# Layer 1 of a four-layer image network: norm sums on 32-column tiles of ones, variances through DRAM, and a new order of work

## The chip, the cores and the metric

The kernel runs on one core of one Trainium2 chip. The metric is the device time of one execution in microseconds (us): the median of several runs, each timed as a whole. A core has five engines with a queue of instructions each: TensorE (PE, with the weight loads, PEld, shown apart), VectorE (DVE), ScalarE (ACT), GpSimd (POOL) and SyncE (SP). SP issues the transfers (DMAs) between DRAM and the on-chip memory. Matmuls write to the accumulation memory, PSUM; the other operands lie in SBUF, both with 128 partitions. An engine works through its queue in order, so an instruction that waits holds up everything queued behind it.

## The reference

Sixteen images of 96 channels and 56 x 56 = 3136 positions pass through four layers. Only the second of them, called layer 1, is touched. It normalises each position over its channels, projects to 192 channels, convolves, runs a selective scan in four directions, normalises again, projects back, and ends with a normalised two-layer perceptron:

```python
def _ln(x, g, b, eps=1e-05):
    m = x.mean(-1, keepdims=True)
    v = ((x - m) ** 2).mean(-1, keepdims=True)
    return (x - m) * jax.lax.rsqrt(v + eps) * g + b
...
z = jnp.transpose(x, (0, 2, 3, 1))
u = _ln(z, norm1_g, norm1_b)
u = u @ in_proj_w.T
...
dt = jax.nn.softplus(jnp.einsum('bkrl,kdr->bkdl', dts, dt_projs_w) + dt_projs_b[None, :, :, None])
a = jnp.exp(dt[:, :, :, None, :] * A[None, :, :, :, None])
bb = dt[:, :, :, None, :] * Bs[:, :, None, :, :] * xs[:, :, :, None, :]
...
_, h = jax.lax.associative_scan(comb, (a, bb), axis=-1)
...
ym = _ln(ym, out_norm_g, out_norm_b)
z = z + ym @ out_proj_w.T
m = _ln(z, norm2_g, norm2_b)
m = jax.nn.gelu(m @ fc1_w.T + fc1_b, approximate=False) @ fc2_w.T + fc2_b
z = z + m
return x + jnp.transpose(z, (0, 3, 1, 2))
```

There are thus three norms per image: the first over 96 input channels, the second over the 192 channels that come out of the scan, the third over 96.

## The kernel before

Layer 0, layer 1 and layers 2 and 3 run one after the other, with their images in DRAM in between. Layer 1 keeps channels in partitions for most of its work and treats one image after another, with neighbouring images overlapping. An image goes through these tasks:

- `front` loads the image in chunks of 896 columns (`loaded`, L1004). Its inner task `sums` squares each piece of 448 columns on ACT (L1029). It then takes 112 columns at a time as weights, with a block of 96 columns of ones/96 as the moving operand: `p_s` (L1035, L1036) holds the mean and the mean square of 112 positions, one position per partition, repeated 96 times. DVE copies out one column of each (L1038), two small operations make the variance (L1044, L1045) and POOL raises it to the power -1/2 (L1047). `projected` loads the chunk again. It spreads the roots over 96 partitions by 28 transposes of a broadcast column (`p_r`, L1057), multiplies (L1062), and projects (L1067). The convolution (L1107) and a silu (L1130) follow. Last, a small projection on four 32-column tiles (L1144, one of its three operands read with a step of 56 elements) is copied to `proj` (L1146), and its rows B and C go to DRAM (`bc`, L1150).
- `made_of` makes the step sizes and decays on PE (L1174) and ACT (L1181, L1183, L1190), and loads the rows of B and C from DRAM, broadcast to 128 partitions (L1203, three buffers `bc`).
- `scanned` is DVE's work: products (L1262, L1265), the scan itself (L1271, L1273) and the product with C (L1226, L1229), in 24 pieces of 784 columns per image. POOL adds directions together (L1295), and at the end DVE folds two halves (L1300). The results are two tiles of an image's size, `y0` (128 channels) and `ym` (64 channels).
- `back` works in seven groups of 448 positions, as three chains. A group squares y on ACT (L1317, L1319). With 112 columns of y as weights it computes the output projection plus one column of means (L1324, L1325), and with 112 columns of squares as weights against ones, the mean squares (L1327). ACT copies the projection out (L1332), DVE makes the variance (L1340, L1341), POOL the power (L1343), DVE scales (L1350) and adds the input image that PE has transposed (`p_y`, L1347, L1352). Then come the third norm (L1357 to L1368), a transpose (L1372), the perceptron (L1382, L1384, L1392, L1393), the last addition (L1395) and the store (L1397).

The order of all this is made by hand while the program is built. Each task is a generator that yields `Op`s: an engine, a guessed cost, a lag until the result can be used, and the buffers that it takes and gives back. `in_order` simulates the engines with these guesses and picks, again and again, the operation with the earliest possible start. Ties go first to an operation that frees PSUM, then to the lower rank. The ranks are `3 * b + -9` for fronts, -100 for `made_of`, 99 for the scan, -1 for the additions and `3 * b` for backs. The instructions are issued in the order of these picks, and on the chip each engine keeps to it. A scanning image and its neighbours share seven image-sized buffers (`big`), three PSUM buffers (`ps`) and single or double buffers of everything else.

```python
            if best is None or (start, rank) < best[:2]:
                best = (start, rank, i)
```

ACT holds one table of functions at a time. The tasks need those of exp (also ln), gelu and silu, and a change costs a table load.

Of the kernel before, what the change touches and what calls it, by code (L numbers as in the profile page):

```python
# [8 lines left out]
F32 = mybir.dt.float32  # L9
# [3 lines left out]
AF = mybir.ActivationFunctionType  # L13
# [150 lines left out]

class Phase:
# [60 lines left out]
def in_order(buffers, tasks, load=None):  # L226
# [8 lines left out]
    def advance(ready, task, parent, root):  # L235
        nonlocal count
        while True:
# [14 lines left out]
            elif isinstance(got, int):  # L252
                ranks[root] = got
            else:
                waiting.append((ready, ("ps" not in got.give, ranks[root], count), task, parent, got, root))
                count += 1
                return
# [3 lines left out]
    while waiting:  # L261
        best = None
        for i, (ready, rank, _, _, op, _) in enumerate(waiting):
            start = max(ready, engines.get(op.engine, 0.0))
            if op.engine == "ACT" and op.table and op.table != tables.get("ACT"):
                start = max(ready, engines.get("ACT", 0.0) + change["ACT"])
# [5 lines left out]
            if best is None or (start, rank) < best[:2]:  # L272
                best = (start, rank, i)
        start, _, i = best
        assert start < np.inf, "the tasks hold all buffers"
        _, _, task, parent, op, root = waiting.pop(i)
# [560 lines left out]
def layer1(ctx, tc, src, given, dst, flags=None, soft=False):  # L837
# [6 lines left out]
    buffers = {  # L844
        "ps": 3, "x": 1, "half": 1, "xc": 2, "big": 7, "proj": 2, "dt": 3, "a": 2, "bc": 3, "hc": 1, "xn": 1,
        "ysq": 1, "o": 2, "z": 2, "zn": 2, "zt": 1, "hid": 1, "xr": 3,
    }
# [28 lines left out]
    ones = ph.c([P, 3, C], "ones")  # L876
# [57 lines left out]
    for i in range(2):  # L934
# [11 lines left out]
        rows.append(ph.c([C1, C], f"rows{i}"))  # L946
        nc.vector.tensor_copy(rows[i], p[:C1, 0, :C])
# [4 lines left out]
    nc.vector.memset(w_out[:, 0, C:], 1.0 / DIN)  # L952
    nc.vector.memset(w_out[:64, 1, C:], 1.0 / DIN)
    for j, n in enumerate((P, 64)):
# [5 lines left out]
        nc.vector.tensor_copy(w_out[:n, j, :C], p[:n, 0, :C])  # L960
    b_fc1 = ph.c([P, 3], "b_fc1")
# [28 lines left out]
    def pe(n, each, take=("ps",), give=(), **k):  # L990
        return Op("PE", n * each, 0.25, take, give, **k)

    def dve(n, each=1.04e-3, over=0.15, **k):
        return Op("DVE", over + n * each, **{"lag": 0.06, **k})

    def act(n, each=0.83e-3, over=0.22, **k):
        return Op("ACT", over + n * each, **k)

    def front(b, it):

        def loaded(g):
            n = min(896, L - 896 * g)
            x = buf([C, 896], "xc")[:, :n]
            nc.sync.dma_start(x, given[b][:, 896 * g : 896 * g + n])  # L1004
            return x
# [15 lines left out]
        me = work.tile([Q, 8, NT], F32, tag="me", name="me")  # L1021

        def sums(g):
            yield Op("SP", 0.3, 4.0, take=("xc",))
            x = loaded(g)
            for i in range(x.shape[1] // T):
                yield act(T, take=("xn",))
                sq = buf([C, 2, T], "xn")[:, 0]
                nc.scalar.activation(sq, x[:, T * i : T * i + T], AF.Square)  # L1029
                last = i == x.shape[1] // T - 1  # L1030
                yield pe(8, 0.2, give=("xn", "xc") if last else ("xn",))
                p = pair("p_s", P)
                for q in range(4):
                    at = T * i + Q * q
                    nc.tensor.matmul(p[:Q, q, :C], x[:, at : at + Q], ones[:C, 0], start=True, stop=True)  # L1035
                    nc.tensor.matmul(p[:Q, 4 + q, :C], sq[:, Q * q : Q * q + Q], ones[:C, 0], start=True, stop=True)  # L1036
                yield dve(8, give=("ps",))
                nc.vector.tensor_copy(me[:, :, 2 * g + i : 2 * g + i + 1], p[:Q, :, 0:1])  # L1038

        yield [sums(g) for g in range(4)]  # L1040
# [837 lines left out]
```

## Time and profile before

| what | value |
|---|---|
| median of 3 runs | 7140.69 us |
| the 3 runs | 7134.35 to 7140.94 us |
| the profiled execution | 7114.45 us |
| its span, first to last instruction | 7112.6 us |
| PE busy | 6280.9 us (88%) |
| DVE busy | 5446.3 us (77%) |
| ACT busy | 4546.6 us (64%) |
| POOL busy | 1446.6 us (20%) |
| mean granted PE clock | 0.92 |
| DMA | 743.56 MB, mean 105 GB/s |

The durations in the prediction come from the one profiled execution. Busy time of an engine is the time in which at least one of its instructions runs. Matmuls overlap one another, so the mean duration of a matmul is longer than its share of PE's time; the distance from one start to the next is the better measure. A line such as `2217.64 0.36 PE L1035 ... x2` in the timeline gives the start, the length, and how many instructions were merged. A line of waits gives who waited for whom, the total in us, the number of times and the longest. In a line of stages, the busy us of each engine are followed by the number of its instructions, the granted PE clock, DMA's mean share and its GB/s.

### The profile page before, as it was taken

What the parts mean: (1) busy time and instruction counts of PE and PEld (TensorE: products, weight loads), DVE (VectorE), ACT (ScalarE), POOL (GpSimd) and SP (SyncE); (2) the same over time, 40 slices, a digit from 0 to 9 for tenths busy, and PEclk for the clock granted to TensorE, in tenths of its full rate; (3) what the DMA queues carried; (4) which work ended last, traced back from release to release, by engine and by line L of the source; (5) the groups of instructions that cost most, each with busy time, mean ns of one, the idle gap of its engine ahead of it and who ended that gap; (6) DMA issues with size and microseconds to landing.
All of it is one profiled execution on the core that took longest, in us unless ns stands there. A gap on an engine that the chain in (4) does not pass through costs nothing. (4 is left out here: it accounts for less than half of the span.)

```text
span 7112.6 us, 114994 instructions
## 1 busy us (share of the span) xinstructions
PE 6280.9 (88%) x46587; PEld 4500.6 (63%) x46587; DVE 5446.3 (77%) x7392; ACT 4546.6 (64%) x6035; POOL 1446.6 (20%) x994
## 2 busy tenths in 40 slices
PE   7999998888889999999999987788999999999986
PEld 3444444445655655556555555687888888888875
DVE  6786884677888888888888885667777777777775
ACT  4454542676777777777777763455666666666664
POOL 0000000132323333333333332111111111111110
PEclk9999998788899999999999988899999999999997
DMA  1111111343444444444444442445555455555542
GB/s 38 31 38 32 40 33 38 110 123 117 124 127 124 127 127 130 127 137 127 128 131 130 126 122 76 96 107 125 130 115 126 112 128 118 121 135 118 119 105 61
DMA packets 495422, 743.56 MB, mean 105 GB/s; under 512 B 199969, under 2 KB 330785, under 8 KB 491570
## 3 DMA queue, kind: packets, MB, share of 16 engines
q1 hardware_dynamic: 493858, 733.25, 39.9%
q8 instruction: 370, 6.06, 0.4%
q0 software_dynamic: 1024, 2.85, 0.1%
q14 instruction: 170, 1.39, 0.1%
HBM read 543.98 MB, written 191.99 MB: 103 GB/s over the span
## 5 line engine op out<-in xcount | busy, mean ns | idle before, releaser
L1578 POOL TENSOR_TENSOR r<-v,nhalf 112x16 f32<-112x16 f32 (+1 forms) x128 | 397.0, 3108 | 2241.5 <-DVE v L1576 1680.7
L1295 POOL TENSOR_TENSOR big<-big,hc 128x784 f32<-128x784 f32 x256 | 537.2, 2099 | 901.9 <-DVE hc L1226 815.2
L1262 DVE TENSOR_TENSOR dt<-dt,big 128x784 f32<-128x784 f32 x384 | 505.5, 1317 | 176.9 <-ACT a L1190 176.7
L777 DVE SCALAR_TENSOR_TENSOR h<-pad,rows,h 128x1568 f32<-128x1568 f32 x288 | 525.9, 1844 | 3.9
L1174 PE MATMUL p_d<-proj,l_dt 32*128 32x392 f32 x1536 | 388.3, 590 | 96.6 <-ACT hid L1384 69.1
L1181 ACT ACTIVATE dt<-p_d,l_dtb 128x784 f32<-128x784 f32 x384 | 350.0, 912 | 128.2 <-PE p_d L1174 110.6
L1636 PE MATMUL p<-k_f,z 112*128 112x112 f32 x3072 | 373.9, 282 | 63.9 <-DMA z<-d 57.5
L1636 PEld LDWEIGHTS p<-k_f,z 112*128 112x128 f32 x3072 | 369.2, 198 | 72.4 <-issue 59.1
L1684 PE MATMUL p_v<-w,gg 128*112 128x97 f32 x2048 | 377.3, 267 | 38.3 <-DVE gg L1670 12.3
L1107 PE MATMUL p_c<-x,taps 64*64 64x392 f32 x4608 | 400.7, 498 | 3.7 <-ACT big L1128 2.7
L1265 DVE TENSOR_TENSOR drive<-dt,bc 128x784 f32<-128x784 f32 x384 | 395.0, 1029 | 11.1 <-DMA bc<-bc 1.0
L1392 PE MATMUL p_g<-l_fc,hid 128*112 128x96 f32 x2688 | 386.1, 285 | 11.8 <-ACT hid L1384 9.4
L1128 ACT COPY big<-p_c 64x392 f32<-64x392 f32 (+1 forms) x448 | 267.3, 599 | 189.7 <-PE p_c L1107 184.1
L1392 PEld LDWEIGHTS p_g<-l_fc,hid 128*112 128x112 f32 x2688 | 347.2, 200 | 51.0 <-ACT hid L1384 24.6
L1685 PE MATMUL p_v<-w2both,gg 128*112 128x97 f32 x2048 | 375.5, 266 | 0.0
L1226 DVE TENSOR_TENSOR hc<-a,bc 128x784 f32<-128x784 f32 x384 | 371.3, 967 | 0.3 <-POOL big L1295 0.2
L1183 ACT ACTIVATE dt<-dt,one 128x784 f32<-128x784 f32 x384 | 363.6, 947 | 7.2
L1382 PE MATMUL p_f<-zt,w_fc 96*128 96x448 f32 x672 | 320.1, 594 | 47.6 <-ACT dt L1181 18.8
L1190 ACT ACTIVATE a<-dt,aneg 128x784 f32<-128x784 f32 x384 | 352.1, 939 | 4.5 <-DVE a L1273 3.1
L750 PE MATMUL p_c<-pad,taps 64*64 64x392 f32 x4032 | 348.8, 495 | 1.8 <-DVE y L816 1.4
L1273 DVE TENSOR_TENSOR_SCAN a<-a,drive 128x784 f32<-128x784 f32 x192 | 350.3, 1824 | 0.1
L1271 DVE TENSOR_TENSOR_SCAN a<-a,drive 128x784 f32<-128x784 f32 x192 | 350.0, 1823 | 0.0
(339 smaller groups left out, 16005.2 us busy)
## 6 DMA issues: line engine op xcount, KB each, us to landing
bc<-bc SPq DMA_DIRECT2D x256, 784.0 KB
bc<-bc SPq DMA_DIRECT2D x256, 392.0 KB
d<-y SPq DMA_DIRECT2D x448, 192.0 KB
z<-d SPq DMA_DIRECT2D x128, 672.0 KB
d<-uu SPq DMA_DIRECT2D x256, 169.8 KB
z<-d SPq DMA_DIRECT2D x192, 194.0 KB
xc<-x SPq DMA_DIRECT2D x96, 336.0 KB
x<-in_x SPq DMA_DIRECT2D x16, 1176.0 KB
```

Source lines behind the costliest of these rows:

```text
L777: nc.vector.scalar_tensor_tensor(out, view, taps9[:, i : i + 1], out, ALU.mult, ALU.add)
L1107: nc.tensor.matmul(p[to : to + 64, b, :TC], taps[64 * s : 64 * s + 64, j, k], pad[64 * s : 64 * s + 64, r0 : r0 + 7, k % 3 : k % 3 + S], s ...
L1174: nc.tensor.matmul(p[:, b, :TC], wdt[on, i], proj[on, h], start=True, stop=True)
L1226: nc.vector.tensor_tensor(hc, a, t[:, 1], ALU.mult)
L1262: nc.vector.tensor_tensor(as_own(dt), as_own(dt), own(u), ALU.mult)
L1265: nc.vector.tensor_tensor(b, dt, t[:, 0], ALU.mult)
L1295: nc.gpsimd.tensor_tensor(out, out, hc, ALU.add)
L1392: nc.tensor.matmul(p[:Q, q, :C], hid[:, j, own], fc2[:, j], start=j == 0, stop=False)
L1578: nc.gpsimd.tensor_tensor(r, v, nhalf[:, :n], ALU.pow)
L1636: nc.tensor.matmul(p[:, q, :Q], flat[:, P * (3 * q + k) : P * (3 * q + k) + P], f2, start=True, stop=True)
L1684: nc.tensor.matmul(out, gs[2 * h][:, at + k], w["w2"][:, 2 * h], start=True, stop=False)
L1685: nc.tensor.matmul(out, gs[1][:, at + k], w["w2both"][:, h], start=False, stop=True)
```

## The change

The first norm becomes a task of its own, `norms`, which writes the roots of an image to a row in DRAM, `root`; `fronts` waits for it. In both the first and the second norm, the block of ones becomes the weight: 32 columns of ones/n on one of four 32-column tiles of PE, with a quarter of the chunk (224, 112 or 196 columns) streaming through each. The sums then lie along the free dimension, the same value in 32 partitions. A new helper, `spread`, squares the means on ACT, makes the variance on DVE and writes one partition of each tile to a DRAM row. Once the row is complete it is loaded again with 28 values in each of 112 partitions, EPS is added and POOL makes all 3136 roots at once. The first norm's roots go back to DRAM and are loaded broadcast over 96 partitions (buffer `xr1`), so that the 28 transposes fall away. The second norm's stay in `r2`, where partition p holds the roots of positions 4p to 4p+3 of each group.

The groups of `back` follow that layout: `each` takes every fourth column of y0, ym and x as weights, so that one partition holds four neighbouring positions. The store then writes them as one piece (`"(p q) c -> p q c"`, before `"(q p) c -> p q c"`). The squares, the ones matmuls, the copy of the projection and the small variance operations leave the group, since the scaling by `r2` reads PSUM directly. `p_y` shares a PSUM tile with `p_o`. The 97th column of `w_out` and `rows` now holds row sums, so that the sum over channels of z comes out of the projection and the reduction L1359 falls away.

A table, TUNED, holds the counts of buffers, the ranks (fronts `3 * b - 6`, the new norms `3 * b - 6`, the scan -50), a handicap for an operation that would change ACT's table (`hold`, 0.7) and a bias in us for some pairs of engine and task (`leads`). `in_order` adds bias and handicap to the start when it picks, not to the simulated time. Some guessed costs change too.

```diff
+            'leads': {('PE', 'spreads'): -2.4,
+                      ('PE', 'steps'): -3.4,
+                      ('SP', 'sums'): -1.2,
+                      ('ACT', 'spreads'): -0.3,
+                      ('DVE', 'additions'): -0.2,
+                      ('ACT', 'hidden'): -0.7,
+                      ('SP', 'norms'): 1.6,
+                      ('POOL', 'fronts'): -0.9,
+                      ('DVE', 'some'): -0.3,
+                      ('POOL', 'norms'): 0.4,
+                      ('PE', 'some'): -0.6,
+                      ('ACT', 'sums'): 0.5,
+                      ('SP', 'projected'): -2.9,
+                      ('DVE', 'norms'): 0.1,
+                      ('POOL', 'backs'): -0.6},
+            'hold': 0.7, 'norm': -6, 'front': -6, 'back': 0, 'make': -100, 'scan': -50, 'chains': 3}}
...
-            start = max(ready, engines.get(op.engine, 0.0))
+            start, key = max(ready, engines.get(op.engine, 0.0)), leads.get((op.engine, name), 0.0)
             if op.engine == "ACT" and op.table and op.table != tables.get("ACT"):
-                start = max(ready, engines.get("ACT", 0.0) + change["ACT"])
+                start, key = max(ready, engines.get("ACT", 0.0) + change["ACT"]), key + hold
...
-            if best is None or (start, rank) < best[:2]:
-                best = (start, rank, i)
+            if best is None or (start + key, rank) < best[:2]:
+                best = (start + key, rank, i, start)
...
-        "ysq": 1, "o": 2, "z": 2, "zn": 2, "zt": 1, "hid": 1, "xr": 3,
+            'ysq': 1, 'vr': 2, 'xr1': 1, 'z': 2, 'zn': 1, 'zt': 1, 'hid': 1, 'xr': 2},
...
+    def spread(mean, square, out, n):
+        yield act(n, take=("vr",))
+        t = buf([P, 224], "vr")[:, :n]
+        nc.scalar.activation(t, mean, AF.Square)
+        yield dve(n, give=("ps",))
+        nc.vector.scalar_tensor_tensor(t, t, -1.0, square, ALU.mult, ALU.add)
+        yield Op("SP", 0.3, 3.0)
+        nc.sync.dma_start(out.rearrange("o (q n) -> (o q) n", q=4), t[::32])
+        yield Op("none", 0.0, 0.0, give=("vr",))
...
+    def normed(b, it):
+        var, it["root"] = (dram.tile([1, L], F32, tag=n, name=n) for n in ("var", "root"))
+        def sums(g):
+            yield Op("SP", 0.3, 4.0, take=("xc",))
+            x = loaded(b, g)
+            n = x.shape[1] // 4
+            yield act(4 * n, take=("xn",))
+            sq = buf([C, 896], "xn")[:, : 4 * n]
+            nc.scalar.activation(sq, x, AF.Square)
+            yield pe(2, n * 1.7e-3, give=("xn", "xc"))
+            p = pair("p_s")
+            for k, a in enumerate((x, sq)):
+                for q in range(4):
+                    nc.tensor.matmul(
+                        p[32 * q : 32 * q + 32, k, :n], ones[:C, 0], a[:, n * q : n * q + n], start=True, stop=True
+                    )
+            yield from spread(p[:, 0, :n], p[:, 1, :n], var[:, 896 * g : 896 * g + 4 * n], n)
...
         def projected(g):
...
-                nc.tensor.transpose(
-                    p[:C, q // 4, Q * (q % 4) : Q * (q % 4) + Q], r[:, at : at + 1].to_broadcast([Q, C]), ident[:Q, :Q]
-                )
-            yield dve(448 * banks, give=("ps", "xc"))
-            nc.vector.tensor_tensor(xn, x.rearrange("c (b n) -> c b n", n=T), p[:C, :banks, :T], ALU.mult)
+            nc.sync.dma_start(rb, it["root"][:, 896 * g : 896 * g + n].to_broadcast([C, n]))
+            yield dve(448 * banks, take=("xn",), give=("xr1", "xc"))
+            nc.vector.tensor_tensor(xn.rearrange("c b n -> c (b n)"), x, rb, ALU.mult)
...
+        def spreads(g):
+            cols = slice(SUB * g, SUB * g + SUB)
+            yield act(SUB, take=("ysq",))
+            sq = buf([P, SUB], "ysq")
+            nc.scalar.activation(sq, y0[:, cols], AF.Square)
+            yield act(SUB)
+            nc.scalar.activation(ym[64:, cols], ym[:64, cols], AF.Square)
+            yield pe(4, n * 1.7e-3, give=("ysq",))
...
+            yield from spread(p[:, 0, :n], p[:, 1, :n], var[:, cols], n)
...
+        each = lambda t, q: t.rearrange("c (p q) -> c q p", q=4)[:, q]
...
-            yield pe(16, 0.2, ("ps", "o"), ("ysq",))
+            yield pe(8, 0.2, ("ps",))
             p = pair("p_o", P)
             for q in range(4):
-                nc.tensor.matmul(p[:Q, q, :C1], y0[:, own], w_out[:, 0], start=True, stop=False)
-                nc.tensor.matmul(p[:Q, q, :C1], ym[:, own], w_out[:, 1], start=False, stop=True)
...
+                nc.tensor.matmul(p[:Q, q, :C1], each(y0[:, cols], q), w_out[:, 0], start=True, stop=False)
+                nc.tensor.matmul(p[:Q, q, :C1], each(ym[:64, cols], q), w_out[:64, 1], start=False, stop=True)
...
+                nc.tensor.matmul(p[:Q, 4 + q, :C1], each(x, q), rows[0], start=True, stop=True)
...
+                z, p[:Q, :4, :C1], r2[:, 4 * g : 4 * g + 4].unsqueeze(2).to_broadcast([Q, 4, C1]), ALU.mult
...
-        in_order(buffers, [fronts(), makes(), scans(), additions(), backs()], None if soft else one_set)
+        in_order(buffers, [norms(), fronts(), makes(), scans(), additions(), backs()], None if soft else one_set, tuned["hold"], tuned["leads"])
```

## The prediction

> **What bounds the kernel now.** I first cut the span into stages. Layer 1 runs from 1152 us, where layer 0 ends, to 4417 us. The busy time by stage shows its head (first image only), its steady part and its tail:
>
> ```profile
> core 0: us, PE busy (x) PEld busy (x) DVE busy (x) ACT busy (x) POOL busy (x), PEclk, DMA share, GB/s
> 1152.00:1282.00 130.00, 96.43 (x704) 59.60 (x704) 14.80 (x61) 37.39 (x51) 12.60 (x29) 0.71 0.11 31
> 1282.00:4085.00 2803.00, 2518.66 (x18722) 1602.23 (x18722) 2365.01 (x2807) 2117.83 (x2752) 902.67 (x644) 0.90 0.44 128
> 4085.00:4417.00 332.00, 272.14 (x1722) 208.97 (x1718) 244.24 (x349) 190.26 (x267) 99.99 (x76) 0.86 0.32 89
> ```
>
> The copy of `proj` (L1146) ends each image's front: its first start is 1281.6 us, its sixteenth 4085.3, so one image takes 2803.7/15 = 186.9 us. The stretch 2007 to 4077 us has PE busy 1899.7, DVE 1791.6 and ACT 1602.0 of 2070 us. That is 171.5, 161.8 and 144.6 us per image, or 92%, 87% and 77% of the period. PE is nearest to full, and DVE is close behind.
>
> Next, what DVE waits for in that stretch, since the scan runs there:
>
> ```profile
> DVE z L1395 <- PE p_g L1393: 115.8, 65, 12.5
> DVE dt L1262 <- ACT a L1190: 79.2, 35, 4.6
> ```
>
> These are 195 of 278 us of DVE's idle time. The first is a wait on PE. The second is a wait on ACT, which itself waits most for PE (p_c 118.1, p_o 103.6, p_d 58.3 us). So PE's load and the hand-made order of the three engines set the period together.
>
> Last, PE's pace. The groups overstate short matmuls, which overlap, so I read starts in the timeline:
>
> ```profile
> 2217.64 0.36 PE L1035 MATMUL p_s<-ones,xc 96*112 96x96 f32 x2
> 2217.83 0.36 PE L1036 MATMUL p_s<-ones,xn 96*112 96x96 f32 x2
> 2218.03 0.36 PE L1324 MATMUL p_o<-w_out,big 128*112 128x97 f32 x2
> 2218.23 0.36 PE L1325 MATMUL p_o<-w_out,big 128*112 128x97 f32 x2
> ```
>
> Each fp32 matmul is two instructions, and the next one starts 0.195 us later: 0.098 us per instruction with its own load of 112 weight columns. After a PE gap the same pair takes 0.37 us (2254.50 to 2254.87) at clock 0.50.
>
> The third reading is what a strided operand costs PE. L1144 runs four 32-column tiles side by side, contiguous ones and ones that read with a step of 224 bytes:
>
> ```profile
> 1278.91 0.12 PEld L1144 LDWEIGHTS p_x<-big,l_xw 128*32 128x32 f32 x4 [0.37 <-issue]
> 1279.24 0.12 PEld L1144 LDWEIGHTS p_x<-big,l_xw 128*32 128x32 f32 x4 [0.21 <-issue]
> 1279.94 0.14 PEld L1144 LDWEIGHTS p_x<-big,l_xw 128*32 128x32 f32 x4 [0.58 <-issue]
> 1280.66 0.14 PEld L1144 LDWEIGHTS p_x<-big,l_xw 128*32 128x32 f32 x4 [0.58 <-issue]
> ```
>
> A new row marks the start of a pass of 392 columns. The contiguous pass took 0.33 us (0.84 ns per column, for four tiles at once), the two strided ones 0.70 and 0.72 us (1.8 ns).
>
> [...] No strided weight load is in this trace. [...] Here the first `bc` rows went to DRAM from 1282.4 and were in use at 1290.3 us, so a write and a read together took at most 7.9 us.
>
> **The change, part by part** (per image, at full clock).
>
> PE, removed: 56 sums matmuls (L1035, L1036) x 0.195 = 10.9 us; 28 transposes of r (L1057, eight instructions in 0.8 us) = 5.6; 56 ones matmuls in the back (L1327) x 0.195 = 10.9. Together 27.4 us.
> PE, added: 32-column tiles in sets of four. The first norm streams 784 columns per tile for x and again for its square; the second 784 for each of two halves of y and their squares. (2+4) x 784 x 2 passes x 0.84 ns = 7.9 us. If the weight loads don't hide, perhaps 12.
> PE, slowed: `each` takes every fourth column, so y0, ym and x are now weights with a step of 16 bytes. Per group that is 8 (p_o) + 4 (p_y) + 4 (L1393) = 16 matmuls, so 32 instructions, and 224 per image. [...]
> Net for PE: -27.4 + 7.9 + 20 = about 0 (bounds -20 and +10).
>
> DVE, removed: seven copies (L1038) 1.15, L1044 and L1045 0.4, L1340 and L1341 (22.2 + 17.7)/16 = 2.5, the reduction L1359 60.8/16 = 3.8. Added: eight `spread` operations on 224 or 196 columns, by the 384-column row of 0.55 us about 0.35 each = 2.8, and two of 28 elements, 0.4. The other two passes over z grow by one column in 97. Net -4.6 us.
>
> ACT, removed: L1332 53.1/16 = 3.3, squares (64.0 + 63.9 + 63.6)/16 = 12.0. Added: four squares of 896 (3.6), eight of 784 (7.4), eight of the means (0.35 each, 2.8). Net -1.5. There are 124 + 111 + 16 = 251 table loads of 1.283 us, 20 us per image. `hold` and `leads` weigh when they come. I take a gain of 1 us of period from order and tables together; bounds -5 to +5, because the trace can't show an order that doesn't exist yet.
>
> POOL: seven powers of 1.39 become one, taken like L1047's 5.1: -4.7, and POOL is 33% busy. The row sums at setup are a few instructions, nothing.
>
> SP and DMA: 15 more DMAs per image (8 row writes, two reads of variances, one write and four broadcast reads of roots), at about 0.4 us of issue = 6 us. SP's existing waits come to about 160 us per image, nearly all for a buffer to come free. Data: 1.2 MB more of broadcasts on DMA engines at 45%. [...] Costed at nothing: three `bc` buffers lie ahead of DVE, which waited 1.0 us for them in all of layer 1. The added waits sit in SP's queue, though: a read of `var` or `root` waits until the write has landed, and the next `bc` rows queue behind it, and L1265 on DVE behind those.
>
> Head: about 33 us from the first p_s (1180) to the first xn (1213) at low clock. Afterwards four loads, three DRAM trips and the power, about 28: -5. Tail: the spreads and the trip come before the last image's first group, about +25 after 4325; each group then loses two squares, a copy, two small operations and a power, some 6 us in 2.3 rounds, and p_o waits less: -20. Together 0.
>
> **Sum.** DVE's 4.6 us less, at its 87% share, shortens the period by 5.3; with 1 for order about 6 us. 15 x 6 = 90. The profiled execution took 7114.45 us (span 7112.6): 7024. The runs' median lies 26 us above it, so 7050.
>
> **Rivals.**
> A, strided weights load at full pace. [...] PE falls to 171.5 - 27.4 + 7.9 = 152 us, DVE at 157.2 becomes the bound; its best long windows show 91.5%, so 172 us: -15 x 15 = -225, 6915.
> B, the slower one: strided loads cost more than L1144's pace. At 0.25 us a load PE gains 30 instead of 20, so +10, 181.5 us. At today's 92% the period is 197: +10 x 15 = +150, 7290. It decides from a load of about 0.23 us on: the forecast's period of 180.9 already has PE at 95%, and at 0.23 (25 gained, 177) PE needs the old period at that share. Against it: the measured strided pace gives 0.20.
> C, SP blocked by the DRAM trips: three per image, 3 us of DVE wait each beyond the cover gives +9 - 6 = +3, +45: 7185. Against it: 1.0 us of wait today.
> D, what goes comes back as other waits: 7140.
>
> **Chances.** Forecast 0.40 (own range 6970 to 7150, 0.05 of it slower), A 0.27, B 0.16, C 0.10, D 0.07. A measurement can tell about 0.2%, 14 us. Faster 0.35 + 0.27 = 0.62, same 0.07, slower 0.05 + 0.16 + 0.10 = 0.31. Range 6850 (A with DVE at 95%) to 7250.
>
> **What would show it.** The distance between weight loads of p_o: 0.1 us gives A, 0.2 the forecast, over 0.23 B. A pass of the new p_s near 0.19 us for 224 columns. DVE near 157 us per image. Waits of L1265 on DMA over 100 us would give C. The forecast falls if the period in the steady part is below 176 or above 187.

## The result, and the profile after

The changed kernel takes 7614.95 us (median of 4 runs, 7610.44 to 7622.51). The kernel before, run beside it, takes 7138.89. The ratio is 1.067, with an interval of 1.065 to 1.0687: 476 us slower, far outside the forecast's range.

The stages of layer 1 in the kernel after (head left out; then steady part, tail, and a stretch inside the steady part):

```profile
core 0: us, PE busy (x) PEld busy (x) DVE busy (x) ACT busy (x) POOL busy (x), PEclk, DMA share, GB/s
1275.00:4452.00 3177.00, 2930.81 (x17758) 1700.63 (x17750) 2274.84 (x2491) 2008.73 (x2557) 803.56 (x553) 0.78 0.40 116
4452.00:4927.00 475.00, 396.72 (x1736) 279.93 (x1734) 285.73 (x349) 206.43 (x264) 110.43 (x77) 0.67 0.28 80
1990.00:4109.00 2119.00, 1981.37 (x11684) 1186.76 (x11681) 1518.46 (x1697) 1326.10 (x1693) 549.23 (x378) 0.79 0.40 115
```

The copies of `proj` (now L1201) start at 1275.0 us for the first image and at 4451.7 for the sixteenth, so the period is 211.8 us instead of 186.9. That makes 15 x 24.9 = 373 us. From the sixteenth copy to the last addition (L1465, at 4921.2) it is 469.5 us instead of 331.3, another 138. The first copy starts 7 us earlier. Together 505 us, of which the span shows 497; the rest is in the other layers.

PE is busy 93.5% of the third stretch. DVE's 1518.46 of 2119 us at this period are 151.8 us per image, fewer than the 161.8 of before: DVE has less to do and waits for PE. The granted clock fell from 0.90 to 0.78. The waits of DVE and ACT between 2000 and 4000 us confirm who is late (total in us, times, longest):

```profile
ACT dt L1236 <- PE p_d L1229: 229.0, 83, 9.7
DVE z L1465 <- PE p_g L1463: 178.8, 59, 6.1
DVE z L1419 <- PE p_o L1416: 150.8, 63, 6.8
DVE dt L1317 <- ACT a L1245: 101.4, 45, 6.0
```

The first was 58.3 us before and is now the longest wait of either engine: the step sizes, on which the scan depends, wait behind PE's other work. The third belongs to an addition that waits for the slowed matmuls themselves.

The pace of these matmuls in the timeline, at full clock until 2018.4 us:

```profile
2010.95 1.70 PE L1122 MATMUL p_in<-xn,w_in 96*128 96x448 f32 x4
2012.48 0.45 PE L1408 MATMUL p_o<-w_out,big 128*112 128x97 f32 x2
2012.86 0.65 PE L1409 MATMUL p_o<-w_out,big 64*112 64x97 f32 x2
2013.44 0.65 PE L1408 MATMUL p_o<-w_out,big 128*112 128x97 f32 x2
2014.02 0.65 PE L1409 MATMUL p_o<-w_out,big 64*112 64x97 f32 x2
...
2016.90 1.97 PE L1416 MATMUL p_o<-rows,xr 97*112 97x97 f32 x8
2018.80 1.68 PE L1229 MATMUL p_d<-proj,l_dt 32*128 32x392 f32 x4
2020.40 3.36 PE L1122 MATMUL p_in<-xn,w_in 96*128 96x448 f32 x4
```

From one start of p_o to the next it is 0.58 us for two instructions, so 0.29 us for each; before it was 0.098. The eight loads of x in L1416 take 1.9 us here and 1.65 us at 2057.69, 0.21 to 0.24 us each. Then something shows that the forecast had no term for: the same four instructions of p_in that took 1.70 us at 2010.95 take 3.36 us at 2020.40. The clock dropped to 0.5 while PE had not been idle for a moment:

```profile
2011.00:2018.30 7.30, 7.30 (x28) 5.88 (x27) 3.74 (x5) 3.34 (x5) 6.18 (x2) 1.00 0.47 146
2018.40:2032.00 13.60, 13.16 (x26) 5.60 (x27) 10.28 (x13) 7.53 (x9) 5.14 (x4) 0.50 0.34 110
```

### The profile page after: what moved, and what is told of

Same layout as the page of the kernel before. It is cut to its first block, busy times and chain, and to the rows that moved or that the text cites. A ratio compares the mean times of both kernels' runs of the same rounds, so it can differ in the third digit from the quotient of the medians.

```text
span 7609.6 us, 112950 instructions
## 1 busy us (share of the span) xinstructions
PE 6789.7 (89%) x45627; PEld 4641.1 (61%) x45627; DVE 5398.6 (71%) x7074; ACT 4458.3 (59%) x5845; POOL 1358.0 (18%) x898
## 5 line engine op out<-in xcount | busy, mean ns | idle before, releaser
L1317 DVE TENSOR_TENSOR dt<-dt,big 128x784 f32<-128x784 f32 x384 | 481.1, 1253 | 186.5 <-ACT a L1245 185.0
L1229 PE MATMUL p_d<-proj,l_dt 32*128 32x392 f32 x1536 | 453.9, 685 | 83.4 <-ACT hid L1454 43.2
L1462 PE MATMUL p_g<-l_fc,hid 128*112 128x96 f32 x2688 | 485.6, 336 | 8.8 <-ACT hid L1454 6.8
L1462 PEld LDWEIGHTS p_g<-l_fc,hid 128*112 128x112 f32 x2688 | 439.0, 247 | 52.5 <-ACT hid L1454 34.5
L1452 PE MATMUL p_f<-zt,w_fc 96*128 96x448 f32 x672 | 373.7, 681 | 34.8 <-ACT zt L1445 14.2
L1320 DVE TENSOR_TENSOR drive<-dt,bc 128x784 f32<-128x784 f32 x384 | 380.0, 989 | 10.3
L1682 PE MATMUL p_a<-first,xt 97*112 97x192 f32 x1792 | 334.9, 334 | 17.2 <-ACT xt L1676 8.1
```

What stands on the lines that cost most here:

```text
L1229: nc.tensor.matmul(p[:, b, :TC], wdt[on, i], proj[on, h], start=True, stop=True)
L1317: nc.vector.tensor_tensor(as_own(dt), as_own(dt), own(u), ALU.mult)
L1320: nc.vector.tensor_tensor(b, dt, t[:, 0], ALU.mult)
L1452: nc.tensor.matmul(p[:, 0, :T], w_fc1[:, P * j : P * j + P], zt, start=True, stop=True)
L1462: nc.tensor.matmul(p[:Q, q, :C], hid[:, j, own], fc2[:, j], start=j == 0, stop=False)
```

## The experiments

Each run is compared with the kernel before on the same chip. The lines named are those of the kernel after.

**1 and 2, the two properties of the loads, one at a time.** The order of the instructions is that of the kernel after in both.

Run 1:

```diff
-        each = lambda t, q: t.rearrange("c (p q) -> c q p", q=4)[:, q]
+        each = lambda t, q: t[:, Q * q : Q * q + Q]
```

Run 2:

```diff
-                nc.tensor.matmul(p[:Q, q, :C1], each(ym[:64, cols], q), w_out[:64, 1], start=False, stop=True)
+                nc.tensor.matmul(p[:Q, q, :C1], each(ym[:, cols], q), w_out[:, 1], start=False, stop=True)
```

> The changed kernel with one edit: the weights of the back's matmuls (p_o, p_y and the rows in p_g) are 112 neighbouring columns instead of every fourth. Every engine keeps the order of the changed kernel, instruction for instruction. The rows of the output then belong to other positions and the second norm's roots to other rows, so this leaves the right assignment out. Theory stride (the strided weight loads take 0.29 and 0.20 us in place of 0.10, and PE's slower clock follows from them): p_o back at 0.10 us per instruction, mean PE clock back to 0.9 in layer 1, and a time of 6850 to 7000 us, below the kernel before. Theory order (the new preferences and the DRAM trips make the loss): the loads get shorter but the time stays above 7300 us.

> The changed kernel with ym's weights over all 128 partitions instead of 64; the lower half of the weight matrix is zero, so that the sum is the same. The order is unchanged. Theory rows (p_o's strided loads take 0.29 us where x's take 0.20 because loads over 128 and over 64 rows alternate and don't overlap the matmul before): p_o falls to 0.20 us per instruction, 112 instructions per image less 0.09 us, some 10 us per image and the clock a little higher, 7400 to 7460 us. Rival (it is something of y's own, its place or its bank): p_o stays at 0.29 us and the time at 7615 us.

Contiguous columns: 7288.03 us, ratio 1.0208 (1.019 to 1.0227), between the ranges of the two theories. 128 rows in every load: 7373.14, ratio 1.0331 (1.0314 to 1.0348), a little under the range of the theory. Taking the step away gains 327 us (7614.95 - 7288.03), and taking the 64 rows away gains 242, although the 64 rows that are added are multiplied by zeros and change nothing in the sum. In the timelines one instruction of p_o takes 0.18 us in run 1 and 0.208 in run 2 (half the distance of the two starts):

```profile
2009.23 0.44 PE L1408 MATMUL p_o<-w_out,big 128*112 128x97 f32 x2
2009.60 0.43 PE L1409 MATMUL p_o<-w_out,big 64*112 64x97 f32 x2
```
```profile
2014.27 0.58 PE L1408 MATMUL p_o<-w_out,big 128*112 128x97 f32 x2
2014.69 0.58 PE L1409 MATMUL p_o<-w_out,big 128*112 128x97 f32 x2
```

The weight loads by themselves, in run 1 with 128 and with 64 rows, then in run 2 (ns; shortest, median and longest of the 896 loads of a line):

```profile
L1408 PEld LDWEIGHTS p_o<-w_out,big x896: 172/176/312, 1503.0 to 4578.4; 128*112 128x112 f32 x180
L1409 PEld LDWEIGHTS p_o<-w_out,big x896: 169/173/308, 1503.3 to 4578.7; 64*112 64x112 f32 x180
```
```profile
L1408 PEld LDWEIGHTS p_o<-w_out,big x896: 278/303/311, 1499.9 to 4658.7; 128*112 128x112 f32 x180
```

With the step a load lasts 0.303 us, without it 0.176. A load of 64 rows lasts as long as one of 128. So in run 1 no load is longer than before (0.178 us there): what grew is the distance from one to the next. The step alone doesn't explain the loss, and contiguous loads still follow each other at almost twice the old distance as long as 128 and 64 rows take turns.

**3, the strided loads in the kernel before** (y0, ym and x as weights with every fourth column, all with their old rows).

```diff
-                nc.tensor.matmul(p[:Q, q, :C1], y0[:, own], w_out[:, 0], start=True, stop=False)
+                nc.tensor.matmul(p[:Q, q, :C1], each(y0[:, cols], q), w_out[:, 0], start=True, stop=False)
```

> The kernel before with one edit: y0, ym and x are read with every fourth column as weights, as in the changed kernel (all 128 rows of ym); the squares keep their columns, so variances belong to other positions and the right assignment is left out. The order of the kernel before is kept. Theory stride: 224 instructions per image at 0.20 us in place of 0.10 are 22 us per image at full clock, and with the clock that falls 7450 to 7600 us. Theory order: PE has slack for it, 7140 to 7250 us.

7359.09 us, ratio 1.0315 (1.0288 to 1.0341): 218 us more, between the two theories, and the clock between 2000 and 4000 us was 0.94 (0.92 in the kernel before). At full clock, 224 loads x 0.108 us x 16 images are 387 us of PE time; 56% of it reaches the end.

**5, both mended, in the order of the kernel after.**

> Both earlier edits of the changed kernel at once: neighbouring columns as weights, and ym's weights over 128 rows. The order is still that of the changed kernel, and the right assignment of positions is left out as in the first run. All weight loads then go at 0.10 us per instruction, so what is left against the kernel before is the order, the smaller set of operations and the DRAM trips. Theory loads (the weight loads are the whole loss): 6900 to 7050 us. Theory loads and order (the new order costs some 150 us or more by itself): 7150 to 7250 us.

7147.49 us, ratio 1.0019 (1.0004 to 1.0034), at the lower edge of the second theory's range. The two properties of the loads are therefore 467 of the 476 us. They don't simply add up: the rows cost 141 us where the loads are contiguous (run 1 - run 5) and 242 where they aren't, and the step costs 226 us with 128 rows throughout (run 2 - run 5) and 327 with 64 rows in turn. The rest of the change, with all that it takes off PE, DVE and ACT, leaves the kernel where it was. Run 10 has the same order on PE, DVE, ACT and POOL and puts every position in its place: the variances come back in 4-byte pieces, and the result leaves by partition and quarter.

```diff
-            v2.rearrange("p (g q) -> p g q", q=4), var.rearrange("o (g p q) -> (o p) g q", q=4, p=Q)
+            v2, var.rearrange("o (m p) -> (o p) m", p=Q)
...
-            nc.sync.dma_start(dst[b][T * g : T * g + T].rearrange("(p q) c -> p q c", q=4), z)
+            nc.sync.dma_start(dst[b][T * g : T * g + T].rearrange("(q p) c -> p q c", p=Q), z)
```

> The kernel after with contiguous columns and 128 rows as in e5, in the same order on TensorE, VectorE, ScalarE and GpSimd, and with the whole result: the variances are read back in 4-byte pieces (28 per partition) so that they fit, and the rows of the result leave by partition and quarter. Theory, the trip through DRAM is hidden and weight loads were the loss: within 1% of e5, 7120 to 7220 us. Rival, the trip decides once its pieces are small: VectorE's wait for the variances (line 1393, 7 us in all so far) grows to more than 10 us per image and the time to over 7300.

7145.05 us, ratio 1.0001 (0.999 to 1.0013), as the theory had it. DVE waited 9.8 us in all for those variances. The strided weights were there so that a partition holds four neighbouring positions. If the DMAs sort the positions instead, it costs nothing that these runs can measure.

**9, the loads by themselves.**

> Nothing of the model is computed here. One core runs nine stages of 240 TensorE instructions each (112 columns of weights taken from one tile of the inputs, 97 moving columns, f32, the shapes of p_o), each after 32 instructions of 448 moving columns. The stages are named by their PSUM tile. Theory: the way the weights lie is what costs. Contiguous, 128 rows (p_near) 0.098 us per instruction; every fourth column, 128 rows (p_far) 0.20 to 0.21; contiguous with 128 and 64 rows in turn (p_near_mixed) 0.18; every fourth column in turn (p_far_mixed) 0.29; 128 and 64 rows in groups of four (p_near_grouped, p_far_grouped) close to the unmixed prices, 0.10 to 0.13 and 0.20 to 0.23; every fourth column with 97 rows (p_far_97) 0.20 to 0.215; every eighth column (p_eighth) like every fourth; every second (p_second) between 0.10 and 0.21. Clock: if slow loads, not idle time, let the clock fall, p_far_mixed shows 0.5 for most of its time, without a gap in TensorE's work, and the stages of 448 columns show 1.0. Rival 1: the prices seen in the kernel come from its neighbours (the order, the DMA traffic); then p_far stays under 0.15 and p_far_mixed under 0.20. Rival 2: the clock falls for another cause; then it is 1.0 in all stages.

This is one execution. The timeline of PE, cut to the nine stages (start, length, tile, shapes; 240 instructions each, so the length divided by 240 is the pace):

```profile
25.31 23.75 PE L1956 MATMUL p_near<-y 128*112 128x97 f32 x240
...
60.95 49.63 PE L1956 MATMUL p_far<-y 128*112 128x97 f32 x240
...
122.47 69.76 PE L1956 MATMUL p_near_mixed<-y 128*112 128x97 f32 x240
...
206.53 77.74 PE L1956 MATMUL p_far_mixed<-y 128*112 128x97 f32 x240
...
298.63 28.61 PE L1956 MATMUL p_near_grouped<-y 128*112 128x97 f32 x240
...
339.30 56.52 PE L1956 MATMUL p_far_grouped<-y 128*112 128x97 f32 x240
...
410.72 49.71 PE L1956 MATMUL p_far<-y 97*112 97x97 f32 x240
...
473.64 24.95 PE L1956 MATMUL p_second<-y 128*112 128x97 f32 x240
...
510.48 50.17 PE L1956 MATMUL p_eighth<-y 128*112 128x97 f32 x240
```

The same run in windows (length; busy us and instructions of PE and of its loads; then the clock):

```profile
122.50:128.40 5.90, 5.90 (x34) 4.38 (x33) 1.00 0.01 3
150.00:180.00 30.00, 30.00 (x99) 21.59 (x99) 0.50 0.00 1
206.60:210.30 3.70, 3.70 (x14) 3.11 (x13) 1.00 0.00 0
230.00:270.00 40.00, 40.00 (x124) 29.54 (x123) 0.50 0.00 0
298.70:320.00 21.30, 21.30 (x180) 19.20 (x180) 1.00 0.00 1
420.00:455.00 35.00, 35.00 (x171) 35.00 (x171) 0.50 0.00 1
511.00:560.00 49.00, 49.00 (x236) 49.00 (x236) 1.00 0.00 1
```

| weights | us per instruction at full clock | at half clock | clock of the stage |
|---|---|---|---|
| contiguous, 128 rows | 0.099 | | stays 1.0 |
| every second column, 128 rows | 0.104 | | stays 1.0 |
| every fourth, 128 rows | 0.207 | | stays 1.0 |
| every eighth, 128 rows | 0.209 | | stays 1.0 |
| every fourth, 97 rows | 0.207 | 0.207 | falls after 4 us |
| contiguous, 128 and 64 rows in turn | 0.18 | 0.30 to 0.31 | falls after 6 us |
| contiguous, in groups of four | 0.119 | | stays 1.0 |
| every fourth, in turn | 0.28 to 0.29 | 0.32 to 0.33 | falls after 4 us |
| every fourth, in groups of four | 0.21 to 0.22 | 0.235 | falls after 4 us |

PE has no gap in any of these stages. The prices in the kernel are those of the loads themselves, not of their neighbours: rival 1 of that run falls.

The price of the rows is a price per change from 128 to 64 or back. In groups of four there is a change after every eight instructions: (28.61 - 23.75)/29 = 0.17 us each. In turn there is one after every two: at full clock these two take 0.365 us contiguous, where two without a change take 0.197, and 0.576 with the step, where two without a change take 0.413. That is 0.16 to 0.17 us again. In the trace of the contiguous stages the load after a change starts 0.27 us after the load before it, any other one after 0.095 to 0.098 us. Whether it starts so late for want of an overlap with the matmul before, as the theory of run 2 had it, no run shows.

And the clock falls in stages that never pause: rival 2 falls too.

**4, 6, 7, 8 and 11, the order.** Run 4 is the whole result with contiguous columns by another way: the variances pass through a PE transpose, which makes the planner find another order. The 64 rows are kept.

> The changed kernel with neighbouring columns as weights, computing the reference: the variances are loaded from their DRAM row as 28 rows of 112 and turned by one PE transpose, and the store writes pieces of 384 bytes again. Theory stride: within 30 us of the first run of this call, 6850 to 7000 us. Theory order: above 7300 us.

7692.76 us, ratio 1.0787 (1.0761 to 1.0813), 405 us more than run 1, whose loads are the same. PE waited only 13.8 us for the DMA that feeds the transposes, so I put the difference down to the order. The 16 added transposes aren't separated from it by a run.

The preferences are `leads`, `hold` and the ranks. Run 6 is run 2 with `leads` empty, `hold` 0 and the old ranks; run 7 is run 4 with 128 rows and these old preferences; run 8 is the kernel before with the new preferences. The edit of run 6 against run 2:

```diff
-            'norm': -6,
-            'front': -6,
+            'norm': -9,
+            'front': -9,
...
-            'scan': -50,
+            'scan': 99,
...
-        in_order(buffers, [norms(), fronts(), makes(), scans(), additions(), backs()], None if soft else one_set, tuned["hold"], tuned["leads"])
+        in_order(buffers, [norms(), fronts(), makes(), scans(), additions(), backs()], None if soft else one_set, 0.0, {})
```

> The changed kernel with ym's weights over 128 rows (7373 us with the new order) and the preferences of the kernel before: no leads, no hold, ranks 3b-9 for norms and fronts and 99 for the scan. The loads stay strided. Theory order (the new preferences are bad for what the chip really takes): 7200 to 7300 us. Rival (they are as good as the old ones, or better): 7373 us or more.

> The fourth run's kernel, which computes the reference with neighbouring columns and a PE transpose of the variances, with ym's weights over 128 rows and the preferences of the kernel before. Theory order: well below the fourth run's 7693 us and below the kernel before, 6900 to 7100 us. Rival (the transpose on PE waits for the DRAM trip and holds up PE's queue, whatever the order): above 7400 us.

> The kernel before with the new picking rule and the new leads, hold and ranks (fronts 3b-6, scan -50), and nothing else of the change; buffers and guessed costs are the old ones, and the leads of tasks that it doesn't have fall away. Theory order: 7250 us or more. Rival (the preferences help, as fewer table loads would): 7000 to 7130 us.

Run 6: 7724.86 us, ratio 1.0819 (1.0779 to 1.0859), 352 us more than run 2. Run 7: 7524.78, ratio 1.0549 (1.0509 to 1.0588). Run 8: 7534.74, ratio 1.0549 (1.0511 to 1.0587), 395 us more than before. In runs 6 and 7 the times of the rivals came, in run 8 that of the theory. The new preferences help the new structure (run 6, with strided loads) and harm the old one (run 8). They don't cause the loss, but they can't be judged apart from the structure. Run 7 changes the rows and the preferences at once, so it doesn't show what either does.

Run 11 tells the planner the prices of the slow matmuls as the trace of the kernel after has them.

```diff
-            yield pe(8, 0.2, ("ps",))
+            yield pe(8, 0.58, ("ps",))
...
-            yield pe(4, 0.2, ())
+            yield pe(4, 0.43, ())
...
-            yield pe(16, 0.2, ("ps",), ("hid", "xr"))
+            yield pe(16, 0.25, ("ps",), ("hid", "xr"))
```

> The kernel after with nothing changed but the prices that the planner of the order is given: 0.58 us for each of the eight matmuls into p_o, 0.43 for each of the four that add the input, 0.25 for the sixteen into p_g, where it had 0.2 for all; the first two are what the trace of the kernel after shows. Theory A, the loads take their time whatever the order: 7500 to 7700. Theory B, a large part of the 476 us is waiting because the order was made with prices less than half of the true ones: 7250 to 7450.

7897.74 us, ratio 1.1055 (1.1022 to 1.1087): both theories miss. An order that is planned with truer prices came out 283 us worse, at a clock of 0.71 between 2000 and 4000 us.

**12, 13 and 14, what sets the period once the loads are mended.** Each leaves out a known amount of one engine's work in run 10 and keeps the order.

```diff
-                for j in range(3):
+                for j in range(1):
                     nc.tensor.matmul(p[:Q, q, :C], hid[:, j, own], fc2[:, j], start=j == 0, stop=False)
```
```diff
-                    nc.vector.tensor_tensor(as_own(dt), as_own(dt), own(u), ALU.mult)
+                    d, n = as_own(dt), as_own(dt).shape[1] // 2
+                    nc.vector.tensor_tensor(d[:, :n], d[:, :n], own(u)[:, :n], ALU.mult)
```
```diff
-                        nc.scalar.activation(dt, dt, AF.Ln, bias=one)
+                        nc.scalar.activation(dt[:, :392], dt[:, :392], AF.Ln, bias=one)
```

> As e10, in the same order, with two of the three products of the second layer of the MLP left out (p_g takes one of three parts of the hidden values): 112 TensorE instructions fewer per image, 11.0 us at 0.098 us each, 176 us in 16 images. Theory A, TensorE no longer bounds the kernel once the loads are contiguous (162 of 185 us busy, half clock included): less than 60 us are gained. Theory B, TensorE still bounds it: 120 us or more. Theory C, the engines bound it in turn, through a fixed order: 60 to 120 us, and each of the three runs gains a part.

> As e10, in the same order, with half of the columns left out where dt is multiplied with the input of the scan: about 20 to 24 VectorE instructions per image shorter by about 0.5 us, 10 to 12 us per image, 160 to 190 us in all. Theory A, VectorE is the bound: 140 us or more are gained. Theory B, TensorE is: less than 40. Theory C, the engines in turn: 40 to 140.

> As e10, in the same order, with half of the columns left out where ScalarE takes the logarithm for dt: about 20 to 24 instructions per image shorter by about 0.35 us, 7 to 8 us per image, 110 to 130 us in all. Theory A, VectorE is the bound: less than 30 us are gained. Theory B, TensorE is: less than 30. Theory C, the engines in turn: 30 to 100.

| run | taken off, 16 images | time | ratio to before | gained on run 10 | share |
|---|---|---|---|---|---|
| 12, PE | 176 us | 7092.97 | 0.9924 (0.9907 to 0.9941) | 52 | 30% |
| 13, DVE | 194 us | 7051.07 | 0.9881 (0.9854 to 0.9907) | 94 | 48% |
| 14, ACT | 126 us | 7116.32 | 0.9968 (0.9954 to 0.9982) | 29 | 23% |

For run 13 the groups between 2000 and 4000 us show the instruction before (run 10) and with half of its columns:

```profile
L1317 DVE TENSOR_TENSOR dt<-dt,big 128x784 f32<-128x784 f32 x250 | 308.1, 1232 | 126.4 <-ACT a L1245 125.3
```
```profile
L1318 DVE TENSOR_TENSOR dt<-dt,big 128x392 f32<-128x392 f32 x257 | 186.6, 726 | 147.9 <-ACT a L1245 146.8
```

It is 0.506 us shorter, 24 times per image, 12.1 us. Of the 121 us that DVE's group lost in this stretch, 22 came back at once as a longer wait for ACT's `a`. By its numbers run 13 says that the engines bind in turn (theory C). Run 12 lies just below the 60 us that I had set for that, which is theory A's answer for PE, and run 14 just below 30. But neither is without effect, though run 14's gain is only just clear of the noise, and no engine gives its relief back in full. I read this as engines that bind in turn, DVE most often.

For run 12 there is another reason beside that. Its clock between 2000 and 4000 us is 0.83, where run 10 has 0.86. By their periods of 181.9 and 184.4 us, PE's busy time fell from 161.7 to 155.4 us per image, 6 us and not the 11.0 taken off at full clock. So a part of PE's relief went to the lower clock and not to another engine. How large a part of the missing 70% that is, no run separates.

**15, 16 and 17, moving work off DVE without leaving any out** (`nc.vector.tensor_tensor` to `nc.gpsimd.tensor_tensor` for xn at L1117, for zn at L1438, and for both).

> As e10 (whole result, same order of the program), but the input of the norm is multiplied with its roots (xn, line 1117) on GpSimd instead of VectorE: about 3.9 us per image leave VectorE (4 instructions of 0.6 to 1.08 us). In e13 half of VectorE's relief came back, so theory C gives 16 x 3.9 x 0.5 = 30 us: 7100 to 7130. Rival: GpSimd is slower (its 128x784 product takes 2.07 us where VectorE's takes 0.98 to 1.23) and its queue stands behind products that wait for the scan (line 1350 waited 628 us in 2000); then p_in waits longer for xn and the time rises above 7160.

> As e10, but z is multiplied with its roots (zn, line 1438) on GpSimd, right behind the power that makes these roots there: 7 instructions of 0.76 us, 5.3 us per image, leave VectorE, and one handover from GpSimd to VectorE goes. Theory C: 16 x 5.3 x 0.5 = 42 us, 7090 to 7125. Rival: the product takes over 1.5 us on GpSimd and delays p_t, and the time stays or rises: 7140 or more.

> Both edits of e15 and e16: 9.2 us per image leave VectorE. Theory C: 16 x 9.2 x 0.5 = 74 us, 7050 to 7110. Rival as there: 7160 or more.

7187.19 us, ratio 1.007 (1.005 to 1.0091); 7143.92, ratio 1.0008 (0.9996 to 1.002); 7186.02, ratio 1.008 (1.0047 to 1.0113). The times are those of the rivals. An xn takes 2.07 us on GpSimd instead of 1.08, and the waits of p_in's matmuls and loads for it grew from 45 to 120 us in all. A zn takes 0.83 us instead of 0.56, not over 1.5 as the rival of run 16 had it, but the waits of p_t's matmuls and loads for it still grew from 106 to 285 us. None of the runs that compute everything is faster than the kernel before; run 10 and run 16 equal it.

## Why the prediction was wrong

**The step that failed** is "PE, slowed", which took 224 loads x 0.09 = 20 us per image. The 0.09 was my estimate from L1144, whose strided moving operand took 1.8 ns per column, 0.202 us for 112 columns, less a part at half clock. No run shows the 20 us: where weights are strided, run 9 showed 0.207 us per instruction, and the kernel after, reckoned at full clock, comes to 33 us per image. As a price of the step of the columns the estimate was good: 0.20 forecast, 0.207 measured with 128 rows. The forecast missed three things, of which the third isn't shown to have cost anything.

- *The rows.* 112 of the 224 loads are p_o's, and they take 128 and 64 rows in turn. Their price is 0.29 us, not 0.20. At full clock the sum is 112 x 0.19 + 112 x 0.108 = 33 us per image in place of 20. The diff shows `ym[:64]`, and the prediction put no cost on it. By itself a load of 64 rows costs no more than one of 128 (0.173 and 0.176 us in run 1). But the price of an instruction didn't follow from the length of its load: with 112 columns in every case the distance went from 0.099 to 0.29 us, by the step, which also lengthens the load (0.303 us in run 2, 0.176 in run 1), and by the changes of rows.
- *The clock.* I reckoned that the step costs almost nothing at half clock. For one load that is about right: with the step it takes 0.207 us at either clock (97 rows, run 9), without it 0.098 and 0.185. But I had no term for a clock that is lower in a kernel with slow loads. Between 2000 and 4000 us the clock was 0.79 in the kernel after, 0.82 in run 1, 0.84 in run 2 and 0.86 in run 5, all in one order of work. In the kernel after it fell 78 times in this stretch, and in 47 of them PE had been busy for over 99.5% of the 3.41 us before.
- *The planner.* It still priced p_o's eight matmuls at 1.68 us (1.05 x 8 x 0.2); they take 16 x 0.29 = 4.6. So the plan has what follows them too early. Whether this is a part of the loss stays open; run 11, meant to show it, made another order that was worse.

With 33 us, rival B's own rule gives (171.5 - 27.4 + 7.9 + 33.4)/0.92 = 201.5 us of period, about 7360 us. So even the right price leaves 255 us, for the clock at 0.78 and the longer tail to explain. Rival B had the right engine and the right direction, with too low a price. Its reason was right only in part: the step alone stayed at L1144's pace (0.207 against 0.202 us), and it was the 64 rows that took p_o's loads past its limit of 0.23 us.

**The error in three parts.** The forecast without any price for the loads was rival A, 6915.

| part | forecast | measured | from |
|---|---|---|---|
| the change with contiguous 128-row loads | 6915 | 7147 | run 5 |
| every fourth column | +135 | +226 | run 2 - run 5 |
| 64 rows in turn | 0 | +242 | after - run 2 |

232 + 91 + 242 = 565, the distance from 7050 to 7615. The last two lines depend on the sequence in which the step and the rows are taken; by run 1 they are +327 - 135 = 192 and +141.

**The first part.** The counts of removed and added work were about right. The new PE passes take 2.8 us (p_s) and 7.5 us (p_v: 16 pairs of passes of 0.47 us), 10.3 instead of 7.9; a single pass of p_s took 0.20 us, as forecast. The stretch from 2000 to 4000 us, in the kernel before and in run 10:

```profile
2000.00:4000.00 2000.00, 1834.40 (x13835) 1197.58 (x13827) 1724.18 (x2105) 1547.09 (x2029) 660.50 (x483) 0.92 0.45 129
```
```profile
2000.00:4000.00 2000.00, 1754.04 (x13131) 994.54 (x13130) 1653.27 (x1831) 1457.56 (x1861) 572.02 (x405) 0.86 0.46 131
```

In run 10 the busy times of PE, DVE and ACT per image are 161.7, 152.4 and 134.4 us (period 184.4). By the same reading the kernel before has 171.4, 161.1 and 144.6. So work went, more than I had forecast for DVE and ACT; ACT's table loads fell from 251 to 189. But the period went from 186.9 to 184.4 only, and the tail grew by 11 us. Two reasons are shown. One: relief of an engine comes back at 30, 48 and 23% (runs 12 to 14), where the forecast passed DVE's relief on in full, and rival A took DVE for the next bound. Two: the clock. Run 10's stretch has 0.86 where the kernel before has 0.92, so of the 17 us taken off PE at full clock (27.4 - 10.3) its busy time shows 10. In both kernels every fall of the clock in this stretch came after a window with pauses of PE (67 falls in run 10, 54 before): with less to do, PE was busy for 1754 of the 2000 us, where it had been for 1834. At those shares the reliefs of about 10, 9 and 10 us would still give some 9 us of period; 2.5 came. What took the other 7 stays open. The added handovers (15 DMAs, PE to ACT to DVE to DRAM and back) and the order are candidates, and the runs don't separate them.

**Other points.** PE was rightly read as nearest to full. The wait for DRAM trips (rival C) didn't come: no product of L1320 (L1265 before) waited on a DMA, and DVE's waits of that kind in layer 1 are 7 us for xn and 7 us for the variances. The head gained nothing where it counts (first product of the scan at 1288.2 us, 1288.3 before) instead of 5 us. The tail was put at 0: from the last product L1317 to the last addition it is 148 us in the kernel after, 108 before, 119 in run 10. So the loads make most of this growth, as the last image's groups consist of little else. The other 98 of the 138 us found above lie ahead of it, where the last scan still runs. Order and tables were given 1 us with bounds of 5; runs 4, 6 and 8 move 350 to 405 us by the order (run 4 with its transposes), or 22 to 25 us per image. That SP waits nearly only for buffers was read too strongly: of the seven longest kinds of its waits between 2007 and 4077 us in the kernel before, 1692 us together, 445 us were stores that waited for z and 92 us were `bc` rows that waited for `proj`, about a third.

## What to carry to other kernels

Before a layout is changed for the sake of a store or a small read, price the matmul that reads it as weights: its column step, and whether loads of different heights follow each other, since 64 rows in turn with 128 were slower here than 128 rows padded with zeros (7615 us against 7373). A plan tuned by hand belongs to the structure that it was tuned for, so a change of one without the other says little about either. Where three engines are each busy for 70 to 90% of a period, don't pass the relief of one on in full: here 23 to 48% of it came back. Measure that share with one run per engine before counting on it.

## What was not expected of the hardware

The clock fell without a pause, and in run 9 just in the four stages that moved the fewest columns and rows per us. Its last dense stage moves 448 columns in 0.377 us (48.30 us for 128 instructions), 0.84 ns per column, so 97 columns take an estimated 0.082 us. Multiplied with the share of the 128 rows and divided by the pace, this gives an estimated use of PE in the nine stages of 83% (contiguous), 79% (every second), 52% (in groups), 40% (every fourth), 39% (every eighth), 34% (contiguous in turn), 30% (every fourth, 97 rows), about 28% (every fourth in groups) and about 21% (every fourth in turn). The first five kept the full clock for the whole stage and the last four lost it within 4 to 6 us. Whether the clock follows this use or something that goes with it, no run shows.

In the traces of the kernels before and after, the times from one change of the clock to the next are multiples of 3.41 us (302 of 303 and 384 of 385). Counted over windows of this length between 2000 and 4000 us, a full-clock window in which PE was busy for less than half was followed by half clock every time: 13 of 13 in the kernel before, 18 of 18 in the kernel after, and likewise in runs 1 to 5. One that was busy for over 99.5% was followed by half clock in 47 of 248 cases in the kernel after, 35 of 301 in run 2, 19 of 278 in run 1 and 11 of 191 in run 4, and in none of 330 in the kernel before, 384 in run 3 and 254 in run 5. Of the windows in between, a part fell in every kernel (41 of 153 in the kernel before). So in these runs the clock fell with pauses in all of them, and without a pause only in kernels with slow loads. Run 3 has strided loads too and kept 0.94. Why, no run shows.

In run 9 the step cost next to nothing at 8 bytes (0.104 us per instruction in place of 0.099), doubled the price at 16 (0.207), and cost hardly more at 32 (0.209).
